# Where the odd bank's start is made in the first 20 turns, and how many images are combined, in a group-norm, quantised-weight convolution

## The chip, the cores and the metric

The kernel runs on one core of a Trainium2 chip. The core has four compute engines with a queue of instructions each: TensorE (PE, the matrix products), VectorE (DVE), ScalarE (ACT) and GpSimd (POOL). SyncE (SP) only issues transfers. Each engine works through its queue in the order in which the program was written, and engines wait for each other at semaphores. The metric is the device time of the core in microseconds (us).

## The reference

`x` has 160 images of 128 channels and 32 x 32 pixels in float32. `U` holds five sets of 128 x 128 x 3 x 3 weights. Cut to what is computed:

```python
def _gn(v, G=32, eps=1e-5):                 # 32 groups of 4 channels
    m, s = mean(g), var(g)                  # per image and group
    return (g - m) / sqrt(s + eps)

s1 = (max(U) - min(U)) / 3.0                # over all five sets
v1 = s1 * floor(U / s1)
s2 = s1 / 5.0
v2 = s2 * floor((U - v1) / s2)
w = (v1 + v2).reshape(128 * 5, 128, 3, 3)
xb = gn(x).reshape(32, 5 * 128, 32, 32)
act = conv(xb, w, stride 1, padding 1, groups=5)
out = x + act.reshape(160, 128, 32, 32)
```

Image `5*b + n` is convolved with set `n`. The kernel takes the images set by set, 32 of each set, and numbers them 0 to 159 in that order.

## The kernel before

**One image.** The 1024 outputs of an image stand in two PSUM banks of 512, "even" and "odd". Normalised pixels are used as two float16 parts, a high one and a low one, so that the product keeps its precision. An image is done in one of two ways:

- A *combined* image (`combined(i)`, L647) has its pixels turned into four quarters of sums and differences of neighbouring columns first: `combine` (L686, L693 on VectorE) and `outer_columns` with a subtraction (L674, L704 on GpSimd) write `v`; ScalarE writes its high part `vh` (L734), VectorE its low part `vl` (L740). Then 24 matmuls do the image.
- Another image, called *direct* here, is normalised to `z` (L710 on GpSimd, or L636 on ScalarE where it is the first of a group of statistics), split into `hi` (L644 on ScalarE) and `lo` (L747 on VectorE); three more VectorE instructions (L760, L768, L769) make `rows` of the low part. It takes 30 matmuls: 18 for `hi` (L784) and 12 for `rows` (L839).

**The two banks.** Four steps fill the banks of an image, by the method names of the code:

1. `begin(i)`: matmuls of the quarter of sums into the even bank: 6 for a combined image, 3 for a direct one.
2. `leave(i)`: ScalarE copies the even bank as it then stands to `half` (L907).
3. `complete(i)`: matmuls of the quarter of differences, added to the even bank: 6 or 3.
4. `odd_from_even(i)`: VectorE writes `odd = 2*half - even` (L914), called "the difference" below.

Then `main(i, 0)` adds the rest to the even bank and `main(i, 1)` the rest to the odd bank: 6 matmuls each for a combined image, 12 each for a direct one. `main(i, 0)` overwrites what the difference reads, and `main(i, 1)` adds to what it writes, so both wait for it.

**Turns.** `run` is a loop over images; turn `i` issues `conv(i)` on TensorE and, on the other engines, steps for images around `i`. Nothing is reordered: the code is under a schedule written by hand. In turn `i` from 4 on, in the order of each engine's queue:

- ScalarE: half of the statistics of images some 10 to 16 ahead (L241), the two evictions of image `i-1` to `sum` (L942, `residual`), the high part of an image 3 or 4 ahead (L734, or L636 and L644), the other half of the statistics (L248), and small copies (`ve` L279, weights L564, first steps of quantising a later set L134).
- VectorE: the low part of an image 2 or 3 ahead (`vl`, or `lo` and `rows`), single steps of quantising the next set of weights (L142 to L146, L162, L544) in between, the difference of image `i+1`, two small instructions on scales (L307, L310), `combine` of an image 4 or 5 ahead, then small statistics (`dv`, L296 to L302) and, for the images in `BY_VECTOR`, whole statistics by VectorE (L231 to L235).
- GpSimd: a power for the scales (L286), `outer_columns` or `z` for an image 4 or 5 ahead, released by the low part on VectorE, and the transfer that adds `sum` to the output (L963).

`step_of` says how far ahead a step is: up to turn 10 the low part is 2, the high part 3 and `combine` 4 images ahead; between turns 11 and 13 each goes one further (`FURTHER = 11`), and the turn in which it changes does two images.

**Order on TensorE.** In turns 4 to 27 it is `begin(i+1)`, `main(i, 0)`, `complete(i+1)`, `main(i, 1)`, with `leave(i+1)` the first instruction of the turn on ScalarE. From `TWO_AHEAD = 28` on (`steady(i)`) `begin` runs two images ahead: `complete(i+1)`, `begin(i+2)`, `main(i, 0)`, `main(i, 1)`; `leave(i+2)` stands behind L241 and ahead of the evictions.

**Which images are combined.** None below 7; those with an odd number from 7 to 29; three of five from 30 to 129; three of four from 130 on.

Of the kernel before, what the change touches and what calls it, by code (L numbers as in the profile page):

```python
# [36 lines left out]
class Later:  # L37
# [25 lines left out]
    def finish(self):  # L63
        run(self.steps)
# [110 lines left out]
def last_of(steps, last=None):  # L175
    for last in steps:
        pass
    return last


def run(steps):

    while True:
        try:
            next(steps)
        except StopIteration as end:
            return end.value
# [134 lines left out]
def general_path(tc, keep, steps, x, u, out):  # L322
# [8 lines left out]
    with tc.If(far > 0), ExitStack() as ctx:  # L331
# [9 lines left out]
        for n in range(N_SETS):  # L341
            un = one.tile([P, C, TAPS], F32, tag="u", name=f"g_u{n}")
            nc.sync.dma_start(un, uv[n])
            wn = one.tile([P, C, TAPS], F32, tag="w", name=f"g_w{n}")
            k1, k2 = run(steps.quantise(one, un, f"g{n}", F32))
            nc.vector.tensor_scalar_mul(wn, k1, steps.s1)
            nc.vector.scalar_tensor_tensor(wn, k2, steps.s2, wn, ALU.mult, ALU.add)
# [38 lines left out]
class Main:  # L386
# [23 lines left out]

    STAT_LEAD = 15
    FURTHER = 11
    TWO_AHEAD = 28
    LOAD_LEAD = 18
    CHUNKS = 11
    STEADY = 7
# [174 lines left out]
    def keep_sums(self, n, col):  # L591
        wt = self.wts[n, col]
        run(self.both_sums(
            self.nc.gpsimd, wt[:, self.SUM], wt[:, self.DIFF], *(wt[:, k] for k in range(ROW))
        ))
# [51 lines left out]
    def combined(self, i):  # L647

        if i < self.STEADY or i >= self.imgs:
            return False  # L650

        if i < self.FIFTHS:
            return i % 2 == 1
        return i % 5 % 2 == 0 if i < self.THIRDS else i % 4 != 2

    def by_scalar_too(self, i):

# [201 lines left out]
    def steady(self, i):  # L859

        return i >= self.TWO_AHEAD

    def conv(self, i, on_the_way):


        ahead = range(i + 1, self.imgs)[:1]
        if self.steady(i) and self.steady(i - 1):
            for k in ahead:
                self.complete(k)
            for k in range(i + 2, self.imgs)[:1]:  # L870
                self.begin(k)
            self.main(i, 0, lambda: on_the_way(self.COLS[1]))
            self.main(i, 1, lambda: on_the_way(self.COLS[2]))
        elif i == self.FIRST:
            self.main(i, 0)
            self.begin(i + 1)
            on_the_way(self.COLS[1])
            self.main(i, 1)
            on_the_way(self.COLS[2])
            self.leave(i + 1)  # L880
            self.complete(i + 1)
        else:
            self.begin(i + 1)
            self.main(i, 0, lambda: on_the_way(self.COLS[1]))
            self.leave(i + 1)
            self.complete(i + 1)
            if self.steady(i):
                self.begin(i + 2)
            self.main(i, 1, lambda: on_the_way(self.COLS[2]))
        del self.v[i]  # L890

# [101 lines left out]
    def run(self):  # L993
# [54 lines left out]
        def measure(stage, *images):  # L1048
            for i in images:
                self.measure(i, (stage,))  # L1050
# [74 lines left out]
        for i in range(self.imgs):  # L1125
# [3 lines left out]
            def on_the_way(col):  # L1129
                if col == self.COLS[1]:  # L1130
                    for st in ready:
                        st.means(self.pg)
                    for *column, parts in self.columns:
                        self.turn_column(*column, parts)
                        turned.append(column)
                    self.columns.clear()
                if col == self.COLS[2]:
                    for st in middle:
                        st.variances()
# [39 lines left out]
            if i < self.FIRST:  # L1179

                if i == 0:
                    measure(0, 8, 9, 10)
                if i == 1:
                    self.normalise(4)
                    self.high_part(4)
                if i == 2:
                    self.normalise(5)
                    measure(1, 9)
                    self.high_part(5)
                    self.odd_from_even(3)  # L1190
                    self.low_part(4)
                    run(self.combinations(4))
                    measure(0, 11)
                self.residual(j)
            else:

                last = None
                for k in self.step_of(i, 2):
                    if self.combined(k):
                        last = last_of(self.low_combined(k), last)  # L1200
                    else:
                        self.low_part(k)
                        later.take(1)
                        last = last_of(self.combinations(k), last)
                last = later.take(1, last)
                if last:
                    before = self.last_but_one(last)
                    for st in scaled:
                        self.after(st.power(), before)
                    for k in self.step_of(i, 4):  # L1210
                        self.beside_pairs(k, before)
                if i > self.FIRST and self.by_hand(j):
                    self.residual(j)
                for k in by_scalar:
                    self.measure(k, (0,))
                if self.steady(i) and i + 2 < self.imgs:
                    self.leave(i + 2)
                if i > self.FIRST and not self.by_hand(j):
                    self.residual(j)
                    self.accumulate(j)  # L1220
                for st in ready:
                    if not st.late:
                        st.deviations()
                for k in self.step_of(i, 3):
                    if self.combined(k):
                        self.high_combined(k)
                        continue
                    if self.by_scalar_too(k):
                        self.normalise(k)
                    self.high_part(k)  # L1230
                for k in by_scalar:
                    self.measure(k, (1,))
# [13 lines left out]

            if i >= self.FIRST:

                if i + 1 < self.imgs:
                    self.odd_from_even(i + 1)  # L1250
                for st in scaled:
                    st.scales_by_vector()
                for k in self.step_of(i, 4):
                    if self.combined(k):
                        self.combine(k)
                    later.take(1)
                later.take_scalar()
                if b in (self.per_set - 4, self.per_set - 2):
                    later.finish()
                for st in ready:  # L1260
                    if st.late:
                        st.deviations_by_vector()
# [65 lines left out]
```

## Time and profile before

| What | Value |
|---|---|
| Median of the runs | 971.14 us (three runs, 970.75 to 971.58) |
| Time of the profiled execution | 971.98 us |
| Its span | 970.2 us |
| TensorE busy | 928.3 us, 96% of the span |
| VectorE busy | 858.9 us, 89% |
| ScalarE busy | 863.3 us, 89% |
| GpSimd busy | 446.0 us, 46% |
| Chain that ended last, TensorE's share | 79% |
| Chain that ended last, ScalarE's share | 10% |
| Chain that ended last, VectorE's share | 5% |
| Mean of one `vh` (L734, ScalarE) | 2024 ns, 94 of them |
| Mean of one `vl` (L740, VectorE) | 2502 ns, 94 |
| Mean of one L686 (VectorE) | 1658 ns, 94 |
| Mean of one `half` (L907, ScalarE) | 577 ns, 157 |
| Mean of one difference (L914, VectorE) | 687 ns, 157 |

The span is what the profile shows from the first to the last instruction; 1.8 us of the profiled execution lie outside it. Busy shares are averages over stages with different limits, so the table alone does not tell what a change in one stage is worth. A matmul's listed duration of some 375 ns overlaps that of the next, since matmuls are pipelined; what one costs in a row of them is the distance from one start to the next. The page lists an engine's idle time in front of a group of instructions with what ended it ("releaser").

### The profile page before, as it was taken

To read this page: it belongs to the slowest core of one execution; us is meant where nothing else is said; L and a number is where in the kernel's file an instruction comes from. 1 tells how busy PE (TensorE), PEld (TensorE's weight loads), DVE (VectorE), ACT (ScalarE), POOL (GpSimd) and SP (SyncE) were. 2 spreads that over 40 slices of the span, in tenths; PEclk is the share of its full clock that TensorE was granted. 3 is DMA by queue.
4 is the path that set the end of the run, shared out by engine and by line. 5 is a ranking of instruction groups with operands and counts; after the bars stand their busy time and mean duration, and the time that the engine had idled before them with its cause. 6 is when DMAs were issued, how large, how long until landed. Compare 5 with 4: busy or idle time off the path is not lost.

```text
span 970.2 us, 12948 instructions
## 1 busy us (share of the span) xinstructions
PE 928.3 (96%) x4432; PEld 434.6 (45%) x4432; DVE 858.9 (89%) x1125; ACT 863.3 (89%) x1320; POOL 446.0 (46%) x481
## 2 busy tenths in 40 slices
PE   2899979999999999999999999999999999999996
PEld 1444434444444444444444444444444444444442
DVE  7988878888899899998999899898989988889973
ACT  5779879998999999999999999999999999997660
POOL 4354433544453443454445444545444455454640
PEclk9999989999999999999999999999999999999998
DMA  9079999999999999999999999999999999756554
GB/s 353 29 270 351 329 353 330 328 326 329 321 314 317 259 283 294 276 284 269 290 252 308 286 282 284 289 277 297 263 274 266 290 280 258 162 90 102 95 93 128
DMA packets 67450, 254.23 MB, mean 262 GB/s; under 512 B 5296, under 2 KB 5296, under 8 KB 67376
## 3 DMA queue, kind: packets, MB, share of 16 engines
q1 hardware_dynamic: 45344, 173.09, 47.8%
q0 software_dynamic: 22032, 80.23, 44.1%
q8 instruction: 37, 0.61, 0.2%
q14 instruction: 37, 0.30, 0.1%
HBM read 89.19 MB, written 164.10 MB: 261 GB/s over the span
## 4 chain that ended last, share of the span: by engine, by line
PE 79%; ACT 10%; DVE 5%; issue 3%; DMA 2%; POOL 1%; SPq 0%; DVEq 0%; ACTq 0%; POOLq 0%
PE even L839 43%; PE odd L839 14%; PE even L784 11%; PE odd L784 11%; ACT junk L248 2%; ACT vh L734 2%; ACT sum L942 2%; ACT junk L241 2%; DMA u<-in_L_conv_U_dram 2%; ACT z L636 1%; ACT half L907 1%; ACT hi L644 1%; DVE ext L508 1%; DVE ext L509 1%; DVE lo L747 1%
## 5 line engine op out<-in xcount | busy, mean ns | idle before, releaser
L839 PEld LDWEIGHTS <-wt 128*128 128x128 f16 x1884 | 184.3, 99 | 211.2 <-issue 4.4
L740 DVE SCALAR_TENSOR_TENSOR vl<-v,rstd,vh 128x2048 f16<-128x2048 f32 x94 | 235.2, 2502 | 48.6 <-ACT vh L734 48.4
L839 PE MATMUL even<-vh,across 128*128 128x512 f16 x564 | 211.3, 375 | 3.5 <-ACT half L907 3.5
L839 PE MATMUL even<-vl,across 128*128 128x512 f16 x564 | 211.3, 375 | 1.7 <-DVE vl L740 1.7
L734 ACT ACTIVATE vh<-v,rstd 128x2048 f16<-128x2048 f32 x94 | 190.2, 2024 | 0.0
L784 PEld LDWEIGHTS <-wt 128*128 128x128 f16 x1242 | 121.7, 100 | 144.2 <-issue 6.6
L248 ACT ACTIVATE junk<-xt,mv 128x1024 uint8<-128x1024 f32 x152 | 176.4, 1160 | 0.3
L839 PE MATMUL even<-rows,wt 128*128 128x512 f16 x567 | 174.2, 381 | 2.5 <-ACT half L907 2.4
L963 POOL DMA_DIRECT2D out_dram<-sum x153 | 135.2, 884 | 89.7 <-ACT sum L942 74.5
L241 ACT ACTIVATE junk<-xt 128x1024 uint8<-128x1024 f32 x152 | 161.2, 1060 | 12.7 <-DMA xt<-in_x_dram 9.8
L839 PEld LDWEIGHTS <-across 128*128 128x128 f16 x1128 | 110.4, 98 | 135.5 <-issue 7.5
L784 PE MATMUL even<-hi,wt 128*128 128x496 f16 (+3 forms) x594 | 162.9, 379 | 4.8 <-DVE odd L914 3.8
L710 POOL TENSOR_SCALAR z<-xt,ngm,rstd 128x1024 f32<-128x1024 f32 x49 | 91.8, 1873 | 152.1 <-DVE rows L769 50.5
L784 PE MATMUL odd<-hi,wt 128*128 128x496 f16 (+3 forms) x594 | 161.0, 375 | 0.0
L686 DVE TENSOR_TENSOR v<-xt 128x960 f32<-128x960 f32 x94 | 155.8, 1658 | 0.5 <-POOL v L674 0.5
L907 ACT COPY half<-even 128x512 f32<-128x512 f32 x157 | 90.6, 577 | 60.1 <-PE even L839 57.1
L674 POOL TENSOR_SCALAR v<-xt,ngm 128x64 f32<-128x64 f32 x94 | 59.0, 628 | 172.8 <-DVE vl L740 74.8
L914 DVE SCALAR_TENSOR_TENSOR odd<-half,even 128x512 f32<-128x512 f32 x157 | 107.8, 687 | 17.3 <-PE even L839 13.8
L839 PE MATMUL even<-vh,wt 128*128 128x496 f16 (+1 forms) x282 | 105.6, 375 | 0.0
L839 PE MATMUL even<-vl,wt 128*128 128x496 f16 (+1 forms) x282 | 105.6, 375 | 0.0
L839 PE MATMUL odd<-vl,wt 128*128 128x496 f16 (+1 forms) x282 | 105.6, 374 | 0.0
L839 PE MATMUL odd<-vh,wt 128*128 128x496 f16 (+1 forms) x282 | 105.6, 374 | 0.0
(148 smaller groups left out, 1131.1 us busy)
## 6 DMA issues: line engine op xcount, KB each, us to landing
xt<-in_x_dram SPq DMA_DIRECT2D x78, 1024.0 KB, 9.6
out_dram<-sum POOLq DMA_DIRECT2D x153, 512.0 KB, 8.8
out_dram<-xt SPq DMA_DIRECT2D x76, 1024.0 KB, 14.2
out_dram<-xt SPq DMA_DIRECT2D x7, 512.0 KB, 6.1
u<-in_L_conv_U_dram SPq DMA_DIRECT2D x4, 576.0 KB, 14.7
xt<-in_x_dram SPq DMA_DIRECT2D x4, 512.0 KB, 9.8
range<-in_L_conv_U_dram SPq DMA_DIRECT2D x3, 576.0 KB, 8.0
u<-in_L_conv_U_dram SPq DMA_DIRECT2D x2, 288.0 KB, 3.0
```

Of the source, the lines that this page charges most:

```text
L241: self.nc.scalar.activation(junk, image, ACTF.Copy, scale=-1.0 / image.shape[1], accum_out=self.mv[:, j, 0:1],)
L248: self.nc.scalar.activation(junk, image, ACTF.Square, bias=self.mv[:, j, 0:1], accum_out=self.mv[:, j, 1:2],)
L674: return self.nc.gpsimd.tensor_scalar(self.view(self.v[i], 0, (512 + W // 2 - 1, 2), (W // 2, H)), self.view(self.image(i), 1, (W - 3, 2), ...
L686: nc.vector.tensor_tensor(self.view(v, 1, (511, 2), (half, H), (1, half - 1)), self.view(x, 1, (1, 2), (W, H), (2, half - 1)), self.view(x ...
L710: ins = nc.gpsimd.tensor_scalar(z, self.image(i), st.ngm[:, j], st.rstd[:, j], ALU.add, ALU.mult)
L734: self.nc.scalar.mul(vh, self.v[i], st.rstd[:, j])
L740: yield self.nc.vector.scalar_tensor_tensor(vl, self.v[i], st.rstd[:, j], self.hi[i], ALU.mult, ALU.subtract)
L784: nc.tensor.matmul(target[a][:, first:end, c0:c1], self.wts[n, col][:, k, :], tile[:, s0 : s0 + 2 * (end - first) - 1 : 2, c0 + dw : c1 + dw],
L839: self.nc.tensor.matmul(out, weights, moving, start=start and j == 0, stop=False, skip_group_check=True)
L907: self.nc.scalar.copy(half, self.eo[i][0])
L914: self.nc.vector.scalar_tensor_tensor(odd, self.half.pop(i), 2.0, even, ALU.mult, ALU.subtract)
L963: added = self.nc.gpsimd.dma_start(self.ov[n, :, b], self.sum.pop(i), accum_op=ALU.add)
```

## The change

Three things change. In turns that are not steady (from turn 4 on), `leave(i+1)` is issued behind the evictions of image `i-1` on ScalarE, `complete(i+1)` behind `main(i, 1)` on TensorE, and the difference of image `i+1` behind the scales, `combine` and the quantising steps of the turn on VectorE. The steady order starts at turn 20 instead of 28. From 30 to 129 five of eight images are combined instead of three of five: 62 instead of 60 of these hundred, and among them every image `i` with `i % 8 == 0`.

```diff
-    TWO_AHEAD = 28
+    TWO_AHEAD = 20
...
-        return i % 5 % 2 == 0 if i < self.THIRDS else i % 4 != 2
+        return i * 5 % 8 < 5 if i < self.THIRDS else i % 4 != 2
...
             self.leave(i + 1)
             self.complete(i + 1)
-        else:
+        elif self.steady(i):
             self.begin(i + 1)
             self.main(i, 0, lambda: on_the_way(self.COLS[1]))
             self.leave(i + 1)
             self.complete(i + 1)
-            if self.steady(i):
-                self.begin(i + 2)
+            self.begin(i + 2)
+            self.main(i, 1, lambda: on_the_way(self.COLS[2]))
+        else:
+            self.begin(i + 1)
+            self.main(i, 0, lambda: on_the_way(self.COLS[1]))
             self.main(i, 1, lambda: on_the_way(self.COLS[2]))
         del self.v[i]
...
                 if i > self.FIRST and not self.by_hand(j):
                     self.residual(j)
                     self.accumulate(j)
+                if i > self.FIRST and not self.steady(i):
+                    self.leave(i + 1)
+                    self.complete(i + 1)
                 for st in ready:
                     if not st.late:
                         st.deviations()
...
-                if i + 1 < self.imgs:
+                if i + 1 < self.imgs and (i == self.FIRST or self.steady(i)):
                     self.odd_from_even(i + 1)
                 for st in scaled:
                     st.scales_by_vector()
...
                     if self.combined(k):
                         self.combine(k)
                     later.take(1)
+                if i > self.FIRST and not self.steady(i):
+                    self.odd_from_even(i + 1)
                 later.take_scalar()
```

## The prediction, made before the changed kernel ran

> **What bounds the kernel now.** I read the busy times by stretch first, then TensorE's (PE's) waits by stretch, then the timelines of PE, VectorE (DVE) and GpSimd around the turns that change. Columns of the first: stretch in us, its length, busy time of PE, PE's weight loads, DVE, ScalarE (ACT), GpSimd (POOL), granted clock, DMA share, GB/s.
>
> ```profile
> 120.00:140.00 20.00, 14.23 (x65) 6.43 (x63) 18.45 (x30) 18.72 (x29) 4.91 (x6) 0.87 1.04 364
> 140.00:160.00 20.00, 20.00 (x92) 9.00 (x91) 15.97 (x25) 13.41 (x21) 6.31 (x8) 0.96 1.04 337
> 180.00:820.00 640.00, 640.00 (x3074) 300.31 (x3073) 585.65 (x738) 616.28 (x949) 301.60 (x303) 1.00 1.01 289
> ```
>
> From 180 to 820 us PE is busy the whole time, and its waits in that stretch are an empty list. What PE saves there, or loses before, reaches the end one to one. Turns 5 to 19 lie between 74.23 us (first matmul of `main(5, 0)`) and 175.06 (that of `main(20, 0)`). PE's waits there, as total, times, longest:
>
> ```profile
> PE even L839 <- ACT half L907: 4.2, 4, 1.8
> PE even L784 <- DVE odd L914: 2.8, 1, 2.8
> PE even L839 <- DVE vl L740: 1.7, 1, 1.7
> ```
>
> Now turn 10's PE timeline (start, us, operation, idle before), and turns 13 and 14:
>
> ```profile
> 107.56 0.38 PE L839 MATMUL even<-rows,wt 128*128 128x496 f16 x1
> 109.76 0.38 PE L839 MATMUL even<-vh,across 128*128 128x512 f16 x1 [1.82 <-ACT half L907]
> ...
> 130.91 0.38 PE L839 MATMUL even<-vh,across 128*128 128x512 f16 x1
> 132.99 0.38 PE L839 MATMUL even<-vl,across 128*128 128x512 f16 x1 [1.70 <-DVE vl L740]
> ...
> 133.83 0.37 PE L839 MATMUL even<-vl,across 128*128 128x496 f16 x1
> 137.00 1.41 PE L784 MATMUL even<-hi,wt 128*128 128x512 f16 x3 [2.79 <-DVE odd L914]
> ```
>
> From 105.22 to 107.56 twelve matmuls start, so one costs 0.2125 us. `main(14, 0)` takes 4.88 us for its twelve (137.00 to 141.88) instead of 2.55: the clock dips (0.87 and 0.96 in the windows, 3.4 us lost of 40, so 6.8 us at half). Turns 5 to 19 hold 411 matmuls of images, 87.3 us of the 100.8. Of the 13.5 left, about 1.5 are the small matmuls of statistics and weights; 12.0 are lost: 8.7 of listed idle time, 2.3 by the clock, 1.0 because a matmul's listed end lies 0.16 behind the next start.
>
> **Part 1: the difference at the end of a turn.** It removes PE's wait for `half` in mid-turn: between `begin(i+1)` and `complete(i+1)` now lie both mains, 2.55 or 5.1 us, which covers the copy (0.58) behind two evictions (0.58 each) and one or two L241 (1.06). Cover gone, it would cost at most today's longest wait, 1.8. The transfer on POOL's queue waits for the evictions, which come earlier by the copy; SP's queue is not passed.
>
> It adds a dependence that runs through every turn. DVE's difference of image i+1 can't start before `complete(i+1)`, PE's last work of turn i; `main(i+1, 0)` can't start before the difference; only `begin(i+2)` lies between. Today `main(i, 1)` lies there too. From the rows: last matmul of a `complete` to the difference 0.49 (110.82 to 111.31), difference to main 0.74 (136.26 to 137.00). From one difference to the next PE needs 0.74 + (n-1) x 0.2125 + 0.49, n being two mains and a `complete`: 7.39 in a turn whose i is even (direct image, n = 30), 4.21 where it is odd (combined, n = 15), 6.76 in turn 5 (n = 27). PE's own work with `begin(i+2)` is 33, 21 and 33 matmuls: 7.01, 4.46, 7.01. So each even turn loses 0.38 even with DVE on time: seven times, 2.7 us.
>
> DVE has to be on time too, and the queue behind its difference is what PE then waits for. What must run between two differences, in turn 9:
>
> ```profile
> 97.71 0.69 DVE L914 SCALAR_TENSOR_TENSOR odd<-half,even 128x512 f32<-128x512 f32 x1 [0.89 <-PE even L839]
> ...
> 98.65 1.28 DVE L231 BATCH_NORM_STATS2 st<-xt 128x6 f32<-128x512 f32 x2
> ...
> 100.34 2.34 DVE L740 SCALAR_TENSOR_TENSOR vl<-v,rstd,vh 128x2048 f16<-128x2048 f32 x1
> 102.60 0.61 DVE L142 SCALAR_TENSOR_TENSOR tt<-nnn,s2nhi,rest 128x384 f32<-128x384 int16 x1
> 103.13 0.68 DVE L914 SCALAR_TENSOR_TENSOR odd<-half,even 128x512 f32<-128x512 f32 x1
> 103.73 1.75 DVE L686 TENSOR_TENSOR v<-xt 128x960 f32<-128x960 f32 x1
> 105.39 0.74 DVE L693 SCALAR_TENSOR_TENSOR v<-xt,twice 128x512 f32<-128x512 f32 x1
> 106.06 0.60 DVE L143 SCALAR_TENSOR_TENSOR tt<-nnn,s2nlo,tt 128x384 f32<-128x384 int16 x1
> ```
>
> By starts: difference 0.60, statistics of image 19 1.69, `vl` 2.26, a quantising step 0.53, L686 1.66, L693 0.67, another step 0.53: 7.94 us, where PE's chain needs 4.21. Today the last three stand behind the difference and PE has `main(i, 1)` to spare. And L686 writes the tile that POOL's L674 wrote just before, which `vl` releases:
>
> ```profile
> 102.86 0.60 POOL L674 TENSOR_SCALAR v<-xt,ngm 128x64 f32<-128x64 f32 x1 [4.24 <-DVE vl L740]
> 103.42 1.03 POOL L704 TENSOR_TENSOR v<-xt 128x512 f32<-128x512 f32 x1
> ```
>
> `vl` ends at 102.68, L674 at 103.46; with no difference in between, DVE waits some 0.2 there, and L686 always runs beside L704. Such a one takes 1.75 (here), one without it 1.16 (at 91.81).
>
> The same sum for the other turns, over PE's own work: turn 5 (statistics 1.68, `vl`, two steps, `combine`) 8.06, over 7.01 by 1.05; turn 7 (`dv` 0.66, `vl`, `combine`, two steps) 6.78, over 4.46 by 2.3; turn 9 by 3.5; turn 11 (`vl`, POOL's power 1.21 behind it, scales 0.7, `combine`) 7.35, by 2.9; turn 13 (`dv`, statistics 1.68, `vl15` and `lo16` with `rows` 5.7) 8.49, by 4.0; turns 14 and 16 (low part, `combine`, steps) 0.2 and 0.5 beyond their 0.38. From turn 14 on the heavy `vl` falls in the even turns, where PE needs 7.39, so turns 15, 17 and 19 lose nothing. With POOL's waits (1.0 in all): 2.7 + 14.4 + 1.0 = 18.1, against 12.0 now: 6.1 us longer. Bounds: with L686 at 1.16 in five turns (-3.0) and no wait for POOL (-1.0) it is +2.2; with L686 at its 1.98 (row at 78.89), that row's wait of 0.49 and L310 at the 0.96 of turn 11, about +9. I take the middle row, 1.75, since L704 is released by the same `vl`.
>
> **The clock.** It dipped behind idle times of 1.70 and 2.79 with six matmuls between, and not behind 1.82 alone. The walk leaves PE idle about 0.6 and 3.05 around the six matmuls of `begin(11)`, 1.1 and 2.75 around those of `begin(15)`, and 2.7 and 2.9 in turns 7 and 11. So none to four dips, each 2.3 (as now, part of it falls into the idle time) to 3.4 (6.8 us at half, all in dense matmuls). I take one at 2.9.
>
> [...]
>
> **Part 2: steady from 20.** Turns 20 to 27 get `begin` two images ahead. PE waits for nothing there today, so I cost it at nothing; what hides it is that `rows` or `vl` of image i+2 are written a turn earlier. Cover gone, `begin(22)` could wait for one low part, 2.3 us at most; no gain is there to take.
>
> **Part 3: 62 combined instead of 60.** Two images with 24 instead of 30 matmuls: 12 x 0.2125 = 2.55 us off PE. DVE gets 2 x (2.50+1.69+0.74 - 1.22-0.68-0.42-0.42) = 4.4 us on top of 585.65 in 640. ACT, the fuller one with 616.28, gets 2 x (2.02-1.07) = 1.9, but loses five L636 of 1.24, since images 48, 56, 88, 96 and 128 open a group and become combined: -4.3. So PE stays the bound. Bounds: 0, if DVE or ACT took over; -4.6, if ACT's relief also ended PE's 1.6 us of waits for `half` and 0.4 of others after 820.
>
> **Sum.** +6.1 + 2.9 + 0 - 2.55 = +6.4 us. The profiled span is 970.2 and its execution 971.98, 0.84 above the median, 971.14; I add to the median: 977.5.
>
> **Rivals.**
> 1. *Short chain, no dip*: part 1 at its low bound: 971.14 + 2.2 - 2.55 = 970.8, no change. For it: two of five L686 in turns 5 to 13 took 1.16. Against: those ran after L704, not beside it.
> 2. *Faster: the free ACT pays.* With the copy behind the evictions ACT never blocks in front of its own work, and the waits for `half` and `vl`, the late difference of turn 14 and the dip all go. At full price only the 2.7 of the even turns stay: 971.14 - 12.0 + 2.7 - 2.55 = 959.3. It decides once all new losses stay below 12.6 us (12.0 + 2.55 - 1.94), that is, if the six DVE-bound turns lose under 10 together, with no dip. For it: DVE idles 2 to 3 us in each even turn. Against: that idle time stands in front of the difference, and DVE's queue is in order (3.6 us idle before the difference of turn 14, with ready work behind).
> 3. *The clock multiplies*: the four stalls dip it, 3 more than in the forecast at 2.5: 985.
> 4. *Part 3 undelivered*: DVE or ACT sets the steady stage: 980.
>
> **How the numbers follow.** Forecast 0.62 (own range 974.5 to 983.5), rival 1 0.13, rival 2 0.11, rival 3 0.10, rival 4 0.04. A change below 0.2% (1.94 us) can't be told from none. Slower: 0.62 + 0.10 + 0.04 = 0.76; same 0.13; faster 0.11. The range takes rival 1 in and leaves most of 2 and 3 out: 970.7 to 983.5.
>
> **What would show it.** In the new profile: no waits for `half` in turns 5 to 19, PE's waits for the difference up from one to a dozen, at 1 to 4 us in turns 7, 9, 11 and 13; DVE without a gap in odd turns up to 13; `main(20, 0)` at 181 (no dip) or later; no PE wait from 190 to 820 and 2.55 us fewer there. I am wrong if the odd turns come in at some 4.5 us, or if DVE's L686 there takes 1.16.

## The result, and the profile after

The changed kernel takes 981.48 us (median of four runs, 980.06 to 983.03) against 970.94 (four runs, 970.43 to 971.58): 1.0108 of the time before, 95% interval 1.0091 to 1.0126. It is 10.5 us longer. The profiled execution is the fastest of the four, 980.06, with a span of 978.3; that of the kernel before, 971.98, is slower than all four of its runs here. So the two profiles, read against each other below, differ by 8.1 us only.

The busy times by stretch of the changed kernel, columns as in the prediction:

```profile
100.00:120.00 20.00, 16.27 (x73) 7.16 (x71) 15.66 (x29) 14.42 (x24) 6.05 (x7) 0.91 1.04 338
120.00:140.00 20.00, 17.04 (x75) 7.75 (x74) 13.79 (x17) 15.69 (x24) 6.32 (x8) 0.91 1.03 362
140.00:160.00 20.00, 16.00 (x69) 6.96 (x68) 18.37 (x31) 13.59 (x20) 6.29 (x7) 0.91 1.04 356
200.00:820.00 620.00, 620.00 (x2982) 291.32 (x2981) 578.66 (x715) 598.51 (x924) 299.33 (x304) 1.00 1.00 283
```

The steady stage is as it was: TensorE has no gap from 200 to 820 us. Before that TensorE is busy 16 to 17 us of 20, ScalarE from 100 to 140 us no longer 19 but 14 to 16, and the clock is below full in three windows instead of two. TensorE's waits from 74 to 185 us (total, times, longest):

```profile
PE even L784 <- DVE odd L917: 12.6, 6, 2.9
PE even L839 <- DVE odd L917: 2.4, 7, 1.1
PE even L839 <- DVE vl L740: 0.8, 1, 0.8
PE small L256 <- DVE mv L235: 0.6, 1, 0.6
```

The waits for ScalarE's copy, 4.2 us before, are gone, and those for the difference (now L917) went from 2.8 us in one place to 15.0 in thirteen. Turn 9 on VectorE, where the difference of image 9 opens the stretch and that of image 10 ends it:

```profile
105.44 0.70 DVE L917 SCALAR_TENSOR_TENSOR odd<-half,even 128x512 f32<-128x512 f32 x1 [2.81 <-PE even L839]
106.04 1.28 DVE L231 BATCH_NORM_STATS2 st<-xt 128x6 f32<-128x512 f32 x2
...
107.73 2.35 DVE L740 SCALAR_TENSOR_TENSOR vl<-v,rstd,vh 128x2048 f16<-128x2048 f32 x1
109.99 0.61 DVE L142 SCALAR_TENSOR_TENSOR tt<-nnn,s2nhi,rest 128x384 f32<-128x384 int16 x1
110.89 1.98 DVE L686 TENSOR_TENSOR v<-xt 128x960 f32<-128x960 f32 x1 [0.28 <-POOL v L674]
112.79 0.74 DVE L693 SCALAR_TENSOR_TENSOR v<-xt,twice 128x512 f32<-128x512 f32 x1
113.45 0.61 DVE L143 SCALAR_TENSOR_TENSOR tt<-nnn,s2nlo,tt 128x384 f32<-128x384 int16 x1
113.98 0.68 DVE L917 SCALAR_TENSOR_TENSOR odd<-half,even 128x512 f32<-128x512 f32 x1
```

From difference to difference it is 8.54 us, with VectorE never idle but for 0.28 behind GpSimd. Over the same time TensorE does `main(9, ...)`, `complete(10)` and `begin(11)`, 4.5 us of work, and waits; then its granted clock is 0.50 from 113.97 to 117.38 us:

```profile
111.45 0.37 PE L839 MATMUL even<-vl,across 128*128 128x496 f16 x1
114.72 1.41 PE L784 MATMUL even<-hi,wt 128*128 128x512 f16 x3 [2.90 <-DVE odd L917]
115.92 0.63 PE L839 MATMUL even<-rows,wt 128*128 128x512 f16 x1
```

114.72 is 0.74 behind the difference's start at 113.98, and the first three matmuls of `main(10, 0)` are 0.4 us apart instead of 0.21. From 114.72 to the first matmul of `main(10, 1)` at 118.56 it is 3.84 us instead of 2.55.

The length of each turn, from the first matmul of `main(i, 0)` to that of `main(i+1, 0)`, read from TensorE's timelines in us; the right-hand columns are experiments, told below:

| Turn | before | after | diff. first | stats by ACT | fillers | both reliefs | FURTHER 12 |
|---|---|---|---|---|---|---|---|
| 4 | 6.78 | 7.78 | 7.78 | 7.78 | 7.79 | 7.79 | 6.79 |
| 5 | 7.02 | 8.66 | 7.02 | 8.21 | 8.67 | 7.02 | 7.02 |
| 6 | 7.16 | 7.54 | 7.54 | 7.54 | 7.54 | 7.54 | 7.16 |
| 7 | 5.20 | 7.23 | 6.55 | 7.23 | 7.23 | 5.44 | 4.95 |
| 8 | 7.02 | 7.40 | 7.40 | 7.40 | 7.40 | 7.40 | 7.02 |
| 9 | 4.59 | 8.53 | 5.80 | 6.85 | 8.53 | 4.59 | 4.59 |
| 10 | 9.15 | 8.83 | 7.54 | 7.53 | 7.53 | 7.65 | 9.14 |
| 11 | 4.45 | 7.36 | 4.45 | 7.35 | 7.36 | 5.28 | 4.45 |
| 12 | 7.33 | 9.38 | 7.70 | 9.37 | 7.70 | 7.71 | 7.33 |
| 13 | 10.85 | 8.48 | 10.21 | 6.80 | 8.49 | 10.70 | 6.62 |
| 14 | 9.35 | 8.74 | 9.69 | 9.08 | 8.17 | 9.01 | 7.06 |
| 15 | 4.45 | 4.45 | 5.87 | 4.45 | 4.45 | 5.86 | 6.57 |
| 16 | 7.02 | 8.29 | 7.40 | 7.40 | 8.28 | 7.40 | 7.02 |
| 17 | 4.45 | 4.45 | 6.27 | 4.45 | 4.45 | 6.27 | 4.92 |
| 18 | 7.16 | 7.54 | 7.53 | 7.54 | 7.54 | 7.54 | 7.16 |
| 19 | 5.61 | 4.75 | 6.12 | 4.75 | 4.75 | 6.12 | 4.76 |

`main(20, 0)` starts at 186.98 instead of 175.06 us, 11.9 later. The first matmul into the odd bank of image 130 comes 9.05 later (812.82 against 803.76), so 2.9 are won back by then, and the span ends 8.1 later.

### The profile page after: what moved, and what is told of

Read it like the earlier page. It is cut to its first block, busy times and chain, and to the rows that moved or that the text cites. A ratio compares the mean times of both kernels' runs of the same rounds, so it can differ in the third digit from the quotient of the medians.

```text
span 978.3 us, 12942 instructions
## 1 busy us (share of the span) xinstructions
PE 929.1 (95%) x4420; PEld 433.8 (44%) x4420; DVE 874.6 (89%) x1118; ACT 862.3 (88%) x1315; POOL 443.0 (45%) x488
## 4 chain that ended last, share of the span: by engine, by line
PE 82%; DVE 8%; ACT 4%; issue 4%; POOL 2%; DMA 0%; DVEq 0%; ACTq 0%; POOLq 0%
PE even L839 44%; PE odd L839 14%; PE even L784 11%; PE odd L784 11%; ACT vh L734 1%; ACT junk L248 1%; DVE vl L740 1%; DVE odd L917 1%; DVE lo L747 1%; ACT sum L945 1%; DVE ext L508 1%; DVE ext L509 1%; DVE st L231 0%; DVE v L686 0%; DVE tt L144 0%
## 5 line engine op out<-in xcount | busy, mean ns | idle before, releaser
L740 DVE SCALAR_TENSOR_TENSOR vl<-v,rstd,vh 128x2048 f16<-128x2048 f32 x96 | 239.4, 2494 | 35.7 <-ACT vh L734 35.6
L839 PE MATMUL even<-vh,across 128*128 128x496 f16 (+1 forms) x576 | 215.8, 375 | 1.7 <-ACT half L910 1.7
L839 PE MATMUL even<-vl,across 128*128 128x496 f16 (+1 forms) x576 | 215.8, 375 | 0.8 <-DVE vl L740 0.8
L734 ACT ACTIVATE vh<-v,rstd 128x2048 f16<-128x2048 f32 x96 | 194.2, 2022 | 1.7 <-DVE v L693 1.7
L784 PE MATMUL even<-hi,wt 128*128 128x496 f16 (+3 forms) x576 | 159.7, 382 | 14.4 <-DVE odd L917 13.6
L686 DVE TENSOR_TENSOR v<-xt 128x960 f32<-128x960 f32 x96 | 167.9, 1749 | 1.7 <-POOL v L674 1.7
L839 PE MATMUL even<-rows,wt 128*128 128x512 f16 x549 | 168.9, 381 | 0.0
L710 POOL TENSOR_SCALAR z<-xt,ngm,rstd 128x1024 f32<-128x1024 f32 x52 | 84.2, 1619 | 164.2 <-DVE vl L740 75.4
L784 PE MATMUL odd<-hi,wt 128*128 128x496 f16 (+3 forms) x576 | 156.3, 375 | 0.0
L674 POOL TENSOR_SCALAR v<-xt,ngm 128x64 f32<-128x64 f32 x96 | 69.0, 718 | 178.8 <-DVE vl L740 103.0
L917 DVE SCALAR_TENSOR_TENSOR odd<-half,even 128x512 f32<-128x512 f32 x157 | 108.2, 689 | 20.8 <-PE even L839 17.1
## 6 DMA issues: line engine op xcount, KB each, us to landing
u<-in_L_conv_U_dram SPq DMA_DIRECT2D x4, 576.0 KB, 12.5
```

The source lines that it names most:

```text
L674: return self.nc.gpsimd.tensor_scalar(self.view(self.v[i], 0, (512 + W // 2 - 1, 2), (W // 2, H)), self.view(self.image(i), 1, (W - 3, 2), ...
L686: nc.vector.tensor_tensor(self.view(v, 1, (511, 2), (half, H), (1, half - 1)), self.view(x, 1, (1, 2), (W, H), (2, half - 1)), self.view(x ...
L710: ins = nc.gpsimd.tensor_scalar(z, self.image(i), st.ngm[:, j], st.rstd[:, j], ALU.add, ALU.mult)
L734: self.nc.scalar.mul(vh, self.v[i], st.rstd[:, j])
L740: yield self.nc.vector.scalar_tensor_tensor(vl, self.v[i], st.rstd[:, j], self.hi[i], ALU.mult, ALU.subtract)
L784: nc.tensor.matmul(target[a][:, first:end, c0:c1], self.wts[n, col][:, k, :], tile[:, s0 : s0 + 2 * (end - first) - 1 : 2, c0 + dw : c1 + dw],
```

## The experiments

**The three parts one by one.** The kernel before of the same chip took 971.65 us in these four.

Part 1 alone: the changed kernel with `TWO_AHEAD = 28` and three of five; the new order holds below turn 20, the old one from 20 to 27.

```diff
-        return i * 5 % 8 < 5 if i < self.THIRDS else i % 4 != 2
+        return i % 5 % 2 == 0 if i < self.THIRDS else i % 4 != 2
...
-    TWO_AHEAD = 20
+    TWO_AHEAD = 28
+    AT_END = 20
...
-                if i > self.FIRST and not self.steady(i):
+                if self.FIRST < i < self.AT_END:
```

> Part 1 alone (new order in turns 4 to 19; steady from 28; three of five combined). Chain theory (the new order alone makes the loss, through the difference that waits behind VectorE's queue): main(20, 0) starts some 11 to 13 us later than before, nothing is won back after, so 11 to 13.5 us longer than the kernel before. Rival (the parts need each other: the earlier steady stage or the new pattern carries some of the loss): under 9 us longer.

Measured: 985.27 us, 1.0139 of before (1.0124 to 1.0155), 13.6 longer. `main(20, 0)` starts at 189.06, 14.0 later than before, but 1.5 of that is there at `main(4, 0)` already (68.95 instead of 67.44), behind a stretch at half clock near 42 us (the mean granted clock is 0.991, in the changed kernel's profile 0.993); turns 4 to 19 are 12.5 longer. Its turns are those of the changed kernel within 0.02 us apart from 10 and 14, where the clock dips fall a little differently (9.21 and 9.08 us).

Part 3 alone: the kernel before with the new line of `combined`.

> Part 3 alone (62 instead of 60 combined). Chain theory: TensorE is the bound from 175 us on, 12 matmuls of 0.2125 us fewer: 2.5 to 2.9 us shorter than before, no wait of TensorE from 190 to 820 us. Rival (VectorE or ScalarE sets that stage, and what the changed kernel won there came with its late start): 0 to 1 us shorter.

Measured: 967.84 us, 0.9962 of before (0.9948 to 0.9976), 3.8 shorter. From 190 to 820 us TensorE waits once, 0.6 us, for the copy. The median gain is above the expected 2.5 to 2.9, and never near 0 to 1. Executions with the same granted clock lie 2.4 to 3.2 us apart on average, close to what was expected (at 0.997, 967.49 and 967.84 against 970.46 and 971.21; at 0.992, 969.35 against 972.24 to 972.82).

Part 2 alone: the kernel before with `TWO_AHEAD = 20`.

> Part 2 alone (steady from 20). Chain theory: TensorE waits for nothing there, so within 0.6 us of before. Rival (the low part is not there for the earlier begin): 1 to 2.5 us longer.

Measured: 971.66 us, 1.0003 of before (0.9994 to 1.0012). Nothing.

Parts 2 and 3 together:

> Parts 2 and 3 without part 1. Chain theory: the sum of the two alone, 2.3 to 3.3 us shorter than before, thus some 13 shorter than the changed kernel. Rival (parts interact): not the sum, longer than before less 1.5 us.

Measured: 968.25 us, 0.9961 (0.9948 to 0.9975), 3.4 shorter. The parts add: 13.6 + 0.0 - 3.8 = 9.8, against 10.5 for all three. The whole loss is part 1, within a us or so.

**What in part 1.** The four that follow change the changed kernel; the kernel before took 971.47 us beside them. Differences "to the changed kernel" compare what the median of each stands above that of the kernel before in its own set (the changed one 10.5).

The difference back ahead of the scales and `combine` on VectorE, with `complete` still last on TensorE:

```diff
-                if i + 1 < self.imgs and (i == self.FIRST or self.steady(i)):
+                if i + 1 < self.imgs:
                     self.odd_from_even(i + 1)
...
-                if i > self.FIRST and not self.steady(i):
-                    self.odd_from_even(i + 1)
```

> The changed kernel with VectorE's difference back ahead of the scales, combine and the steps behind it; complete stays behind both mains on TensorE. Chain theory (what VectorE must run between two differences sets the odd turns): turns 5, 7, 9 and 11 come down to TensorE's own 7.0 or 4.5 to 5.1 (minus 1.6, 2.8, 3.4, 2.9), turn 16 by 0.9, while combine moves into the next turn: turn 13 grows by about 2.3, turns 15, 17 and 19 by 1.2, 2.6 and 1.1; with one or two clock dips gone, 4 to 8 us shorter than the changed kernel. Rival (TensorE's own order, complete behind both mains, makes the loss): within 1.5 us of the changed kernel.

Measured: 974.48 us, 1.0025 of before (1.0014 to 1.0036): 7.5 of the 10.5 us gone. (The table shows less, 4.5 us in turns 4 to 19: the profiled execution is the slowest of its eight, 975.84, and keeps a dip of 6.8 us in turns 13 and 14: the granted clock is 0.94 from 120 to 140 us and 0.89 from 140 to 160.) Turns 5, 9, 11, 16 fall to 7.02, 5.80, 4.45 and 7.40, turns 13, 15, 17 and 19 grow by 1.7, 1.4, 1.8 and 1.4, as `combine` now stands in them. Turn 7 comes down by 0.7 only and not by 2.8: there TensorE now waits for something else.

```profile
94.59 0.81 PE L839 MATMUL even<-rows,wt 128*128 128x512 f16 x3 [1.81 <-ACT half L910]
```

This row of that kernel's TensorE timeline is `complete(8)`. With VectorE out of the way ScalarE is the next to be late in that turn, which the expectation did not have. In turn 9, 5.80 instead of the expected 4.5 to 5.1, TensorE waits 0.95 us for a statistic of VectorE.

The statistics of images 14, 19, 24 and 29 by ScalarE:

```diff
-    BY_VECTOR = (8, 10, 11, 14, 19, 24, 29, 34)
+    BY_VECTOR = (8, 10, 11, 34)
```

> The changed kernel with the statistics of images 14, 19, 24 and 29 by ScalarE instead of VectorE (1.69 us less in VectorE's queue in turns 5, 9, 13 and 16, some 2.5 us more on ScalarE in turns 4, 8, 12 and 15). Chain theory: turns 5, 9, 13 and 16 shorter by 1.65, 1.7, 1.7 and 0.9, and the clock dips of turns 10 and 14 gone or not: 5.5 to 9 us shorter than the changed kernel. Rival (ScalarE is the bound of these turns, as the waits for the copy said of the kernel before): 2 us or more longer, with waits of TensorE for the copy.

Measured: 974.54 us, 1.0029 of before (1.0020 to 1.0039), 7.5 shorter than the changed kernel. Turns 9 and 13 lose 1.68 us each, what the instructions cost (1.69 and 1.68), and turn 16 loses 0.89, down to TensorE's own 7.40; no wait for ScalarE's copy appears, although ScalarE got some 10 us of work. In the table turns 4 to 19 are 5.7 us shorter in all. Turn 5 falls by 0.45 only, since VectorE then stands in front of GpSimd:

```profile
80.57 1.98 DVE L686 TENSOR_TENSOR v<-xt 128x960 f32<-128x960 f32 x1 [1.52 <-POOL v L674]
```

Nine matmuls without use ahead of `begin` in the waits of turns 7, 9, 11 and 13, into the odd bank that the difference fills afterwards:

```diff
+    FILLED = (8, 10, 12, 14)
+    def fill(self, i):
+        zeros = self.los[3].rearrange("p h w -> p (h w)")
+        self.filled = odd = self.bank_of(self.ps_odd, i)
+        for _ in range(9):
+            self.nc.tensor.matmul(odd..., zeros[:, :128], zeros[:, :512], start=True, stop=True)
...
                 if i > self.FIRST and not self.steady(i):
+                    if i + 1 in self.FILLED:
+                        self.fill(i + 1)
                     self.odd_from_even(i + 1)
```

> The changed kernel with nine matmuls without use, into the odd bank before the difference fills it, in the waits of turns 7, 9, 11 and 13: TensorE stays busy there. Clock theory (three half-clock windows cost 1.3 to 1.5 us each on top of the waits): no dip before the end, main of 10, 12 and 14 at 2.55 us each, 3.5 to 4.5 us shorter than the changed kernel. Rival (the dips fall into time that is waited anyway): within 1 us; or the nine matmuls delay the difference: longer.

Measured: 977.30 us, 1.0059 of before (1.0042 to 1.0076), 4.7 shorter than the changed kernel, a little more than expected. Its TensorE timeline (the filler is L912, the difference L930):

```profile
111.41 2.11 PE L912 MATMUL odd<-lo 128*128 128x512 f16 x9
...
115.74 0.80 PE L784 MATMUL even<-hi,wt 128*128 128x512 f16 x3 [0.96 <-DVE odd L930]
```

The wait behind the filler is short, the three matmuls take 0.80 us instead of 1.41, and the turns in which TensorE waits (5, 7, 9, 11, 13) are as long as they were. From 100 to 120, 120 to 140 and 140 to 160 us the granted clock is 1.00, where the changed kernel has 0.91 three times. In the table turns 10, 12 and 14 are 1.3, 1.7 and 0.6 us shorter, 3.6 in all: that is the price of the three dips.

The copy back at the head of ScalarE's turn, with the rest of part 1 as changed:

```diff
             self.begin(i + 1)
+            self.leave(i + 1)
             self.main(i, 0, lambda: on_the_way(self.COLS[1]))
             self.main(i, 1, lambda: on_the_way(self.COLS[2]))
+            self.complete(i + 1)
...
-                if i > self.FIRST and not self.steady(i):
-                    self.leave(i + 1)
-                    self.complete(i + 1)
```

> The changed kernel with the copy back at the head of ScalarE's turn, ahead of L241 and the evictions; complete and the difference stay at the end. Chain theory (TensorE does not wait for the copy once complete is last): within 1 us of the changed kernel, a little longer if ScalarE now waits in front of its other work. Rival (the copy behind the evictions is what sets the turns): 3 us or more shorter.

Measured: 982.05 us, 1.0108 of before (1.0091 to 1.0125): no difference to the changed kernel. Where the copy stands on ScalarE does not matter once `complete` is last.

**How far can it go?** The kernel before took 971.39 us beside these four. Both reliefs at once, the difference first and the statistics by ScalarE:

> The changed kernel with both reliefs of VectorE's queue: the difference ahead of combine, and the statistics of images 14, 19, 24, 29 by ScalarE. Chain theory: the two gains add where they touch different instructions: turn 13 at some 8.5 us (10.2 without the second relief), turn 9 at 4.5 to 5.0, turn 5 at 7.0, the clock dip of turn 14 perhaps gone: 971 to 973, so still no faster than the old order with parts 2 and 3 (968.3). Rival (the new order was held back by VectorE's queue alone): 967 or less.

Measured: 972.83 us, 1.0013 of before (1.0004 to 1.0023), with parts 2 and 3 in it; the old order with them has 0.9961. Turns 5 and 9 are at TensorE's own 7.02 and 4.59. Turn 13, expected at 8.5, stays at 10.70: TensorE waits 2.7 us there for a small statistic of VectorE, 0.5 for ScalarE's copy, and 2.4 for the difference at its end. VectorE had itself stood 2.1 us idle in front of that statistic, behind ScalarE:

```profile
131.29 0.16 DVE L296 TENSOR_SCALAR twice<-small 128x4 f32<-128x4 f32 x1 [2.08 <-ACT wt L564]
```

The copy also costs 0.7 us each in turns 7 and 11. So VectorE's queue held the new order back, but not alone.

The old order loses 12 us before turn 20 as well, 8.7 of them in turns 13 and 14 (10.85 and 9.35 against 4.46 and 7.01 of matmuls). In turn 13 the low part goes one image further ahead, so VectorE does two of them. Three kernels with the old order and part 3 shift that turn:

```diff
-    FURTHER = 11
+    FURTHER = 12
```

> The old order with part 3 and FURTHER = 12 instead of 11: the turn that does two low parts is 14 (direct image first) and no longer 13, the two combines come in turn 12. Chain theory: the 12 us that the old order loses before turn 20 sit mostly in turns 13 and 14 (10.85 and 9.35 us against 4.46 and 7.01) because two low parts and statistics stand in front of the difference of an odd turn; in an even turn TensorE has 7 us: 3 to 8 us shorter than with part 3 alone (967.8), the dip gone. Rival (ScalarE's lateness in turns 10 to 13 makes that stall): within 1.5 us of 967.8.

Measured: 964.12 us, 0.9923 of before (0.9907 to 0.9940), 7.3 shorter, 3.5 more than part 3 alone. It is the fastest kernel of the study. TensorE's waits from 74 to 187 us:

```profile
PE even L784 <- DVE odd L914: 2.3, 2, 2.0
PE even L839 <- ACT half L907: 2.0, 2, 1.8
PE even L839 <- DVE vl L740: 1.8, 1, 1.8
```

Behind the waits of 1.8 and 2.0 us that end at 132.38 and 147.15, matmuls start 0.21 us apart, as they do at full clock, and turns 13 and 14 take 6.62 and 7.06 us; turn 15 gives 2.1 back. In the profiles turns 4 to 19 are 5.2 us shorter than with part 3 alone, whose profiled execution has the dip in turn 14 (mean granted clock 0.995, here 0.996); the medians show the 3.5.

> As before with FURTHER = 13: the two low parts in turn 15, an odd turn again, but with no whole statistics by VectorE beside them, two combines in turn 13. Chain theory: a stall in turns 15 and 16 of some 3 to 5 us in place of the 8.7 of turns 13 and 14: 2 to 5 us shorter than 967.8. Rival: within 1.5 us.

Measured: 967.68 us, 0.9959 (0.9945 to 0.9973): nothing over part 3 alone, as the rival had it. Turns 13 and 14 are short (5.74 and 7.58), but 15 and 16 take 8.84 and 9.15, with a dip of 6.8 us (mean granted clock 0.993). The stall only moved, which the expectation had too small.

> As before with FURTHER = 14: the two low parts in turn 16, an even turn, with the statistics of image 29 in front of them. Chain theory: 2 to 7 us shorter than 967.8, less than with 12 since the odd turns before it stay loaded with vl and combine (low part 2 ahead) longer. Rival: within 1.5 us.

Measured: 966.16 us, 0.9942 (0.9925 to 0.9959), 5.2 shorter, 1.4 more than part 3 alone: less than the expected 2 to 7 and inside the rival's 1.5: turns 15, 16 and 17 take 7.54, 7.57 and 6.33, without a dip (mean granted clock 0.998).

## Why the prediction was right, and where its sizes were off

- *The loop.* "DVE's difference of image i+1 can't start before `complete(i+1)` ... `main(i+1, 0)` can't start before the difference." That is what the changed kernel does. The even turns without more came at 7.40 and 7.54 (with a statistic's matmuls) for 7.39, the odd ones with VectorE on time at 4.45 for 4.46.
- *VectorE's queue.* Forecast for turns 5, 7, 9, 11, 13 and 16: 8.06, 6.78, 7.94, 7.35, 8.49 and 7.9. Measured: 8.66, 7.23, 8.53, 7.36, 8.48, 8.29. Moving one group of instructions out (the difference first, the statistics by ScalarE) moved the turns that hold it, and the median of the kernel by 7.5 us each. Turn 14, put at 0.2 over 7.39, came at 8.17 where no dip disturbed it (fillers): VectorE waits 0.95 there for GpSimd's power, and L310 takes 0.95 instead of the 0.16 it took in the old turn 14.
- *L686, mis-sized.* The middle price, 1.75 us, was taken with a wait of 0.2 for GpSimd; it ran at the high bound, 1.98, behind a wait of 0.28, in turns 5, 7, 9 and 16. This GpSimd view shows why:

```profile
110.26 0.59 POOL L674 TENSOR_SCALAR v<-xt,ngm 128x64 f32<-128x64 f32 x1 [7.22 <-DVE vl L740]
110.82 1.03 POOL L704 TENSOR_TENSOR v<-xt 128x512 f32<-128x512 f32 x1
```

  L686 starts at 110.89, when L704 has just begun, so it shares all of L704's time and not the last 0.7 us of it. The wait that the forecast itself put in front of L686 made the row at 78.89 (a wait, then 1.98) the nearer one. Over the 94 L686 of the old profile the duration goes with the time shared with L704: 1.14 to 1.17 us at 0.1 or less, 1.31 at 0.3, 1.52 at 0.5, 1.64 to 1.80 at 0.6 to 0.8, 1.98 to 2.01 at 1.0. In turns 5, 7, 9 and 16 together this and the waits make 2.0 us over the forecast's sums, of which 1.0 had been put in as POOL's waits.
- *Turn 11, right by luck.* Its 7.36 for 7.35 is two errors that cancel. The scales (L307 and L310, 127.14 to 128.44) took 1.30 us instead of 0.7, as they had in the old turn 11; so L686 came when L704, at 127.46 for 1.03, was all but over, and took 1.15 instead of 1.75:

```profile
127.14 0.38 DVE L307 TENSOR_SCALAR rstd<-rstd,lift 128x4 f32<-128x4 f32 x1 [0.93 <-POOL rstd L286]
127.56 0.96 DVE L310 TENSOR_TENSOR shift<-ngm,rstd 128x4 f32<-128x4 f32 x1
128.44 1.15 DVE L686 TENSOR_TENSOR v<-xt 128x960 f32<-128x960 f32 x1
129.50 0.74 DVE L693 SCALAR_TENSOR_TENSOR v<-xt,twice 128x512 f32<-128x512 f32 x1
```

  "L686 always runs beside L704" does not hold there, and the sign of being wrong, L686 at 1.16, showed in this turn although the cause was right.
- *The clock, mis-sized.* One dip at 2.9 us was taken, from none to four at 2.3 to 3.4. There were three, in turns 10, 12 and 14 (bounds right), at 1.3, 1.7 and 0.6 us. Each is 3.413 us at half clock, half of the 6.827 us of the old trace's dip. TensorE's longest wait in these turns was 2.9 us.
- *Turn 4, left out.* The sum began with turn 5, but turn 4 has the new order too: 7.78 instead of 6.78 us. 0.38 of it is the even turn's loss (three matmuls of `begin` do not cover the difference). The rest is `main(4, 1)`, which comes earlier and now waits for a small statistic of GpSimd:

```profile
71.76 0.38 PE L273 MATMUL small<-dv,gavg 128*128 128x4 f32 x2 [0.60 <-POOL dv L270]
```

- *The copy.* Costed at nothing with the mains as cover: right, since placing it first or last made no difference (982.05 and 981.48).
- *Part 2* at nothing: right (1.0003, 0.9994 to 1.0012).
- *Part 3, mis-sized.* 2.55 us from 12 matmuls, measured 3.8 as a median. In the two profiles 2.9 are won between turn 20 and image 130: the matmuls, and 0.3 us at two places (334.39 and 560.81 us) where the old kernel's `complete` started 0.36 and 0.38 us behind the matmul before it instead of 0.21; no wait is listed there, and the changed kernel has one such place, at 800.57. The spans add a difference behind the last matmul: from its end to the last instruction it is 8.3 us in the old profile, 7.7 in part 3 alone and 7.4 in the changed kernel, but 6.8 to 8.3 over all fourteen profiles, with and without part 3, so it is not shown to belong to the change. As far as the runs show, the rest of the 3.8 is which dips the executions happened to have: those with the same granted clock lie 2.4 to 3.2 us apart on average.
- *The sum.* Part 1 with its clock was put at 9.0 us and is 11.9 in the profile (1.0 for turn 4; beyond the forecast, 1.0 for L686 and the waits, 0.6 for turn 14 and 0.7 for the dips; 0.4 less for small matmuls) and 13.6 by the medians alone. The medians also hold dips that differ from run to run: three of the four runs of the changed kernel have a granted clock of 0.991 instead of the profiled 0.993, and are 1.2 to 3.0 us longer. So +10.5 instead of +6.4, inside the range and with the cause named, 4 us too short. Of the rivals, "short chain" and "the free ACT pays" fell with VectorE's rows; "the clock multiplies" was half right in number and wrong in price. What the free ScalarE won, 4.2 us of waits for the copy, is real; 15.0 us of waits for the difference came in their place.

## What to carry to other kernels

Before a step is moved to the end of a turn, close the loop: follow what the next turn's first work waits for, and add up each engine's queue between two passes of that point; the longest sum sets the turn, and cover that lay between two steps is gone once they are neighbours. An average load of 80 to 90% on an engine says nothing where its heavy turns coincide with the short turns of the engine that sets the end: shifting a step by one turn (`FURTHER = 12`), so that it falls in a long one, won 3.5 us with no instruction saved. And count the clock in: in the changed kernel three dips, each behind 3.41 us in which TensorE was busy for 0.66 to 1.26, cost 3.6 us on top of the waits.

## What was not expected of the hardware

In the changed kernel's trace TensorE's granted clock is 0.50 in three stretches between 30 us and the last matmul: from 113.97 to 117.38, 131.03 to 134.45 and 148.10 to 151.52 us, each 3.413 us long, and 17.06 and 17.07 us from start to start. In the trace of the kernel before it is 0.50 in one, from 134.94 to 141.77 us, 6.827 us long. From 114.72 us on, at half clock, matmuls start 0.40 to 0.43 us apart; at full clock it is 0.21. TensorE's busy time in the 3.41 us ahead of each dip, and in the first 3.41 us of it:

| Kernel | Dip begins, us | Its length | Busy in the 3.41 us ahead | Busy in its first 3.41 us |
|---|---|---|---|---|
| before | 134.94 | 6.827 | 1.21 | 1.35 |
| changed | 113.97 | 3.413 | 1.26 | 2.66 |
| changed | 131.03 | 3.413 | 0.66 | 3.41 |
| changed | 148.10 | 3.413 | 1.21 | 2.76 |

With the same two profiles cut into stretches of that length from a dip's start, forward and back between 62 and 170 us, the other stretches at full clock have TensorE busy for 1.53 us or more: 1.53 from 96.90 to 100.32 us in the changed kernel and 1.59 from 107.63 to 111.05 in the kernel before are the lowest, and behind both the clock stays at 1.00. In the changed kernel the wait of 2.48 us that ends at 98.79 is in no dip and has none behind it; those of 2.90, 2.75 and 2.80 that end at 114.72, 130.90 and 148.76 have the three. In the kernel before a wait of 1.82 us has none (it ends at 109.76), and 1.70 and 2.79 with six matmuls between have one. With the fillers, nine matmuls more in each of four waits, the granted clock is 1.00 from 100 to 160 us and the longest wait 1.8. Whether the length of a wait or the busy time of a stretch sets a dip off, these rows do not tell.

The granted clock differs from run to run, and the time with it: of the seventeen runs of the kernel before in the second set, seven with a granted clock of 0.992 took 971.74 to 972.65 us, six at 0.994 took 970.92 to 971.77, and four at 0.996 or 0.997 took 970.14 to 970.55. Those last clocks leave no room for the dip of turns 13 and 14, which takes 0.0035 off the mean, beside the fall behind the last matmul (0.50 from 964.38 us to the end of the span, another 0.0030). A dip near 42 us, as in the profile of part 1 alone, is there before the turns begin (`main(4, 0)` at 68.95 instead of 67.44 us); what sets it off is open.
